# Score products over 128 rows: padding a 64-row contraction with zeros

## The chip, the core and the metric

The kernel runs on one core of a Trainium2 chip. A core has a matrix engine (TensorE, PE in the profile, with its weight loads as PEld), a vector engine (VectorE, DVE), a scalar engine (ScalarE, ACT), a general engine (GpSimd, POOL) and a sync engine (SyncE, SP) that here issues most of the DMAs. Each has its own queue of instructions and runs it in order; semaphores tie the queues together. The metric is the time on the device in microseconds (us), as the median of three executions. The profile is of one execution of its own.

## The reference

Two layers on an image batch x of 4 x 512 x 32 x 32, in float32. Each normalises its input over groups of channels and adds its output to it.

Layer 0 is a state-space mixer over the 1024 positions. Layer 1, in which the change lies, is attention over positions between two 3x3 convolutions:

```python
x_top = _conv(x, w_top, b_top, 0)           # 512 -> 64 channels, 1x1
x_center = _conv(x, w_center, b_center, 0)  # 512 -> 64 channels, 1x1
x_bottom = _conv(x, w_bottom, b_bottom, 1)  # 512 -> 512 channels, 3x3
sp_map = einsum('bnp,bpm->bnm', x_center^T, x_top)   # p: 64 channels
sp_map = softmax(sp_map over all n and m)
sp_map = einsum('bnm,bmc->bnc', sp_map, x_bottom^T)
out = _conv(x + sp_map.reshape(...), w_out, b_out, 1)
```

The score product is the first einsum: per image a 1024 x 1024 matrix, contracted over the 64 channels p.

## The kernel before

Layer 0 fills about the first 2190 us. A planner written in Python (`Plan`, with costs and due times) fixes its order; the change does not touch it, and its order on every engine stays as it was.

Layer 1 is written in program order and ordered by the compiler's scheduler. Its main loop (lines 1476 to 1488) runs over the four images b:

- `scores(0)` for the first image, once, ahead of the loop
- `conv3("b..")`: the bottom convolution, as a Winograd transform. Inputs `e`, `f`, `g`, `h`, `k`, `l` are made on ScalarE and GpSimd (lines 1331 to 1351), summed into `rr` and `v` on VectorE (1335, 1336, 1370 to 1373), and multiplied on TensorE with weights `uw` (line 1383, results `m_b`), which SyncE streams in 1 MB pieces through three buffers (line 1379). `n` (VectorE) and `y` (GpSimd, lines 1403 to 1418) gather the results
- `norm(b + 1)`: loads and normalises the next image, with the edges of its padded copy `xg` set to zero by GpSimd (lines 223 to 226)
- `attend`: scores times `y` (line 1431, `pat`), added to the image
- `scores(b + 1)`: the scores of the next image
- `conv3("o..")` (results `m_o`) and `finish`, the output convolution; `finish` loads the residual into `o` tiles (line 1457), transposes on TensorE (line 1464, `po`) and writes out (line 1474)

So the scores of image 0 stand ahead of its bottom convolution, and those of images 1, 2 and 3 ahead of the output convolution of the image before.

`scores` first makes both 1x1 convolutions in one product (line 1242, `pt`): 128 output rows, of which 0 to 63 are `top` and 64 to 127 `center`. ScalarE adds the biases and writes each into a tile of 64 partitions (lines 1247 and 1254); `center` comes from the upper half of PSUM into partitions 0 to 63. Then come 16 score products per image (line 1263, `psc`), each with 128 columns of `top` as weights and 512 columns of `center` streamed, over 64 rows. ScalarE copies each result to `st` (line 1267), VectorE takes row maxima `mx` (1268) and their maximum `mp` (1271), GpSimd the maximum over partitions (1273), and ScalarE the exponentials (1277).

`top` and `center` take two of three buffers of one ring, "f4" in the pool `l1f`; the `o` tiles of `finish` (128 partitions, the same length) share it. So a `top` or `center` of image 2 or 3 waits until an `o` tile has been written out, and an `o` tile until the score products that read `top` or `center` are done. A buffer costs the same space per partition whether a tile uses 64 partitions or 128.

Of the kernel before, what the change touches and what calls it, by code (L numbers as in the profile page):

```python
# [8 lines left out]
F32 = mybir.dt.float32  # L9
AF = mybir.ActivationFunctionType  # L10
# [5 lines left out]
P = 128  # L16
B, C, HH, WW = 4, 512, 32, 32
L = HH * WW
# [5 lines left out]
T = 512  # L24
NH = L // T
NB = B * NH
PAB = 64
# [143 lines left out]
def mamba_then_pab_kernel(  # L171
# [25 lines left out]
    nc = tc.nc  # L197
# [18 lines left out]
    pb_sb = cpool.tile([P, 1], F32, tag="pb", name="pb_sb")  # L216
# [952 lines left out]
    with ExitStack() as l1:  # L1169
# [5 lines left out]
        TI, TJ = HH // 4, WW // 2  # L1175
# [7 lines left out]
        fp = l1.enter_context(tc.tile_pool(name="l1f", bufs=3))  # L1183
# [50 lines left out]
        def scores(b, xg):  # L1234


            top = fp.tile([PAB, L], F32, tag="f4", name=f"top_{b}")
            center = fp.tile([PAB, L], F32, tag="f4", name=f"center_{b}")
            for h in range(NH):
                pt = ps.tile([P, T], F32, tag="ps", name=f"pt_{b}_{h}")  # L1240
                for c in range(NCC):
                    nc.tensor.matmul(
                        pt, wt_sb[:, c].rearrange("p j n -> p (j n)"),
                        xg[:, c, 1 + h * HR : 1 + (h + 1) * HR, 1 : WW + 1],
                        start=(c == 0), stop=(c == NCC - 1),
                    )
                nc.scalar.activation(
                    center[:, h * T : (h + 1) * T], pt[PAB:P], AF.Identity, bias=pb_sb[PAB:P]
                )
                tv = top.rearrange("p (r k i j) -> p r i j k", r=4, k=2, j=TJ)  # L1250
                pv = pt[0:PAB].rearrange("p (i r j k) -> p r i j k", r=4, j=TJ, k=2)
                hi = slice(h * TI // 2, (h + 1) * TI // 2)
                for r in range(4):
                    nc.scalar.activation(
                        tv[:, r, hi], pv[:, r], AF.Identity, bias=pb_sb[0:PAB]
                    )
            mx = spool.tile([P, NMC], F32, tag="mx", name=f"mx_{b}")
            st = []
            for m in range(NMC):
                t = xp.tile([P, L], F32, tag="st", name=f"st_{b}_{m}", bufs=NMC)  # L1260
                for h in range(NH):
                    pt = ps.tile([P, T], F32, tag="ps", name=f"psc_{b}_{m}_{h}")
                    nc.tensor.matmul(  # L1263
                        pt, top[:, m * P : (m + 1) * P], center[:, h * T : (h + 1) * T],
                        start=True, stop=True,
                    )
                    nc.scalar.copy(t[:, h * T : (h + 1) * T], pt)
                nc.vector.reduce_max(mx[:, m : m + 1], t, axis=AX.X)
                st.append(t)
            mp = spool.tile([P, 1], F32, tag="mp", name=f"mp_{b}")  # L1270
            nc.vector.reduce_max(mp, mx, axis=AX.X)
            ma = spool.tile([P, 1], F32, tag="ma", name=f"ma_{b}")
            nc.gpsimd.partition_all_reduce(ma, mp, P, bass_isa.ReduceOp.max)
            nc.vector.tensor_scalar_mul(ma, ma, -1.0)
            rs = spool.tile([P, NMC], F32, tag="rs", name=f"rs_{b}")
            for m in range(NMC):
                nc.scalar.activation(
                    st[m], st[m], AF.Exp, bias=ma, accum_out=rs[:, m : m + 1]
                )
            rp = spool.tile([P, 1], F32, tag="rp", name=f"rp_{b}")  # L1280
            nc.vector.reduce_sum(rp, rs, axis=AX.X)
            return st, rp
# [192 lines left out]

        xg = image[0]
        st, rp = scores(0, xg)
        for b in range(B):
            xb = conv3(f"b{b}", xg, ub, brow[0])
            after = norm(b + 1) if b + 1 < B else iter(())  # L1480
            next(after, None)

            v, chunk = by_chunk(f"o{b}", xg) if b + 1 == B else (None, None)
            attend(b, xg, st, rp, xb, after, chunk)
            if b + 1 < B:
                st, rp = scores(b + 1, image[b + 1])
            finish(b, conv3(f"o{b}", xg, uo, brow[1], v))
            xg = image.get(b + 1)
# [57 lines left out]
```

## Time and profile before

Three executions took 3271.97, 3272.30 and 3289.61 us. The profiled one took 3276.93, of which its trace spans 3275.1.

| part of the span | length us | PE busy | DVE busy | ACT busy | POOL busy | PEclk |
|---|---|---|---|---|---|---|
| to 2191 (layer 0) | 2191.0 | 1821.5 | 1651.9 | 1761.3 | 1978.4 | 0.92 |
| from 2191 (layer 1) | 1084.1 | 1051.0 | 540.1 | 146.1 | 286.2 | 0.95 |

How to read it: PEclk is the share of TensorE's full clock that was granted, averaged over the stretch. In layer 1 TensorE is busy 97% of the time, the other engines half of it at most. TensorE's waits there are few: 6.3 us before the score products of the four images together (for `top`), 5.1 before `po`, 4.1 before `m_o` (for `v_o`), 3.8 before `m_b` for weights.

### The profile page before, as it was taken

The numbers are of one execution on the slowest core, as the hardware profiler recorded it, in microseconds if no ns is written. First come the engines' busy times: TensorE is split into PE (matmuls) and PEld (weight loads), VectorE is DVE, ScalarE is ACT, GpSimd is POOL, SyncE is SP. The second block draws the span as 40 slices with busy tenths as digits, with TensorE's granted clock in tenths as the row PEclk, the third lists the DMA queues.
The fourth block names the chain that finished last, engine by engine and source line by source line (L and its number), as shares of the span: only waits on it lengthen the run. The fifth ranks groups of instructions, "written<-read, shape, count | busy, mean of one in ns | idle before, by whom it ended". The sixth has DMA issues, their size and how long they took to land.

```text
span 3275.1 us, 35019 instructions
## 1 busy us (share of the span) xinstructions
PE 2872.5 (88%) x11416; PEld 1688.1 (52%) x11416; DVE 2192.0 (67%) x1837; ACT 1907.4 (58%) x3589; POOL 2264.5 (69%) x1240
## 2 busy tenths in 40 slices
PE   5988688889778988888898978689999999999998
PEld 3545565555555655556655566554444444444443
DVE  3557788875888876789876599875365446447444
ACT  3389889996898986799998689752030030021000
POOL 7889989998899897899999799762142133224122
PEclk9889799999989998889999989798989989999999
DMA  7678868899778798968889888755438618808916
GB/s 231 172 269 311 272 213 269 282 317 323 272 242 264 270 304 293 326 224 262 283 292 324 293 302 284 219 203 214 166 137 314 241 59 310 324 32 299 327 72 251
DMA packets 388125, 823.81 MB, mean 252 GB/s; under 512 B 48360, under 2 KB 220136, under 8 KB 363368
## 3 DMA queue, kind: packets, MB, share of 16 engines
q1 hardware_dynamic: 378848, 806.01, 72.6%
q10 hardware_dynamic: 8936, 15.31, 1.3%
q8 instruction: 91, 1.49, 0.2%
q14 instruction: 90, 0.74, 0.1%
q0 software_dynamic: 160, 0.26, 0.0%
HBM read 720.28 MB, written 101.19 MB: 251 GB/s over the span
## 4 chain that ended last, share of the span: by engine, by line
PE 43%; POOL 22%; DVE 9%; DMA 8%; issue 7%; ACT 7%; SPq 0%; POOLq 0%; DVEq 0%; ACTq 0%
PE m_o L1383 10%; PE m_b L1383 9%; POOL da L818 7%; PE pat L1431 7%; POOL bbc L792 5%; PE y L826 4%; PE po L368 4%; POOL bbc L818 3%; PE psc L1263 3%; DVE da L806 2%; DMA bbc<-bcd 2%; ACT sc L763 2%; DVE bbc L806 2%; DMA cbc<-bcd 2%; DMA uw_b<-u_b 2%
## 5 line engine op out<-in xcount | busy, mean ns | idle before, releaser
L806 DVE TENSOR_TENSOR_SCAN da<-da,u 128x1024 f32<-128x1024 f32 x256 | 582.5, 2276 | 152.8 <-PE u L777 151.5
L763 ACT ACTIVATE sc<-dtxt,bt_sb 128x128 f32<-128x128 f32 x2048 | 633.2, 389 | 57.2 <-PE u L777 57.0
L792 POOL TENSOR_TENSOR bbc<-dtx,bbc 128x1024 f32<-128x1024 f32 x256 | 604.3, 2371 | 59.4 <-DMA bbc<-bcd 43.8
L818 POOL TENSOR_TENSOR da<-da,cbc 128x1024 f32<-128x1024 f32 x256 | 604.8, 2364 | 55.5 <-DVE da L806 48.0
L826 PE MATMUL y<-ident,da 128*128 128x128 f32 x2048 | 304.6, 296 | 127.1 <-POOL da L818 120.0
L826 PEld LDWEIGHTS y<-ident,da 128*128 128x128 f32 x2048 | 249.7, 152 | 238.6 <-POOL da L818 208.5
L806 DVE TENSOR_TENSOR_SCAN u<-u,bbc 128x1024 f32<-128x1024 f32 x128 | 292.2, 2283 | 103.3 <-ACT u L798 71.7
L826 PE MATMUL y<-ident,bbc 128*128 128x128 f32 x2048 | 303.0, 294 | 64.1 <-POOL bbc L818 38.0
L777 PE MATMUL u<-ident,sc 128*128 128x128 f32 x2048 | 300.7, 293 | 53.0 <-DVE da L806 33.9
L771 ACT ACTIVATE da<-dt,a_sb 128x1024 f32<-128x1024 f32 x256 | 290.5, 1140 | 92.0 <-PE y L826 91.3
L1383 PE MATMUL m_b<-uw_b,v_b 128*128 128x512 f32 x768 | 338.0, 598 | 6.8 <-DMA uw_b<-u_b 3.8
L1383 PE MATMUL m_o<-uw_o,v_o 128*128 128x512 f32 x768 | 339.0, 603 | 4.1 <-DVE v_o L1305 4.1
L806 DVE TENSOR_TENSOR_SCAN bbc<-u,bbc 128x1024 f32<-128x1024 f32 x128 | 291.8, 2280 | 55.5 <-ACT u L798 42.8
L826 PEld LDWEIGHTS y<-ident,bbc 128*128 128x128 f32 x2048 | 255.1, 152 | 126.5 <-POOL bbc L818 69.6
L818 POOL TENSOR_TENSOR bbc<-bbc,cbc 128x1024 f32<-128x1024 f32 x128 | 302.6, 2364 | 24.5 <-DVE bbc L806 22.1
L798 ACT ACTIVATE u<-dt,a_sb 128x1024 f32<-128x1024 f32 x256 | 284.6, 1112 | 54.5 <-DVE da L806 22.8
L777 PEld LDWEIGHTS u<-ident,sc 128*128 128x128 f32 x2048 | 255.9, 152 | 116.1 <-issue 37.6
L368 PE MATMUL pz<-xt,winc 128*128 128x512 f32 x512 | 249.2, 615 | 8.0 <-DVE xs L618 2.9
L1383 PEld LDWEIGHTS m_o<-uw_o,v_o 128*128 128x128 f32 x768 | 147.8, 193 | 195.6 <-issue 186.0
L1383 PEld LDWEIGHTS m_b<-uw_b,v_b 128*128 128x128 f32 x768 | 144.2, 191 | 194.5 <-issue 179.7
L1431 PE MATMUL pat<-y_b,st 128*128 128x512 f32 x512 | 221.7, 593 | 0.1
L1391 ACT ACTIVATE e_b<-m_b 128x512 f32<-128x512 f32 x24 | 14.3, 597 | 328.5 <-PE m_b L1383 299.3
(225 smaller groups left out, 4263.6 us busy)
## 6 DMA issues: line engine op xcount, KB each, us to landing
cbc<-bcd SPq DMA_DIRECT2D x512, 512.0 KB, 5.4
bbc<-bcd SPq DMA_DIRECT2D x256, 512.0 KB, 5.9
uw_b<-u_b SPq DMA_DIRECT2D x96, 1024.0 KB, 5.4
uw_o<-u_o SPq DMA_DIRECT2D x96, 1024.0 KB, 4.8
u_b<-work SPq DMA_DIRECT2D x192, 128.0 KB, 2.8
u_o<-work SPq DMA_DIRECT2D x192, 128.0 KB, 4.9
szd<-sz SPq DMA_DIRECT2D x32, 512.0 KB, 6.8
szl<-szd SPq DMA_DIRECT2D x32, 512.0 KB, 5.9
```

What stands on the lines that cost most here:

```text
L368: lambda k=k, lhs=lhs, rhs=rhs: nc.tensor.matmul(p()[:, :cols], lhs(), rhs(), start=(k == 0), stop=(k == n - 1)),
L763: nc.scalar.activation(sc()[:, k, :], dtxt()[:, k, :], AF.Copy, scale=bt()[:, k, s : s + 1],)
L771: lambda: nc.scalar.activation(da(), dt(), AF.Exp, scale=scale),
L777: nc.tensor.transpose(u()[:, k * P : (k + 1) * P], sc()[:, k, :], ident)
L792: "POOL", 2.38, lambda: nc.gpsimd.tensor_mul(dbx(), dtx(), b_bc()),
L798: lambda: nc.scalar.activation(da(), dt(), AF.Exp, scale=scale),
L806: lambda: nc.vector.tensor_tensor_scan(ht(), da(), dbx(), 0.0, ALU.mult, ALU.add),
L818: "POOL", 2.38, lambda: nc.gpsimd.tensor_mul(hc(), ht(), c_bc()),
L826: nc.tensor.matmul(y[h]()[:, k, :], hc()[:, at * P : (at + 1) * P], ident, start=(s == 0 and k == 0), stop=(s == NS - 1 and k == NK - 1), ...
L1263: nc.tensor.matmul(pt, top[:, m * P : (m + 1) * P], center[:, h * T : (h + 1) * T], start=True, stop=True,)
L1383: nc.tensor.matmul(m[q], v[:, q, k, c, :], w[:, c, :], start=(c == 0), stop=(c == NCC - 1 and not extra),)
L1431: nc.tensor.matmul(pt, st[m][:, 2 * P * j + h : 2 * P * (j + 1) : 2], xb[m // 2][:, m % 2, :], start=(m == 0), stop=(m == NMC - 1),)
```

## The change

The tiles `top` and `center` grow from 64 partitions to all 128. GpSimd sets their partitions 64 to 127 to zero, with two memsets of 64 x 1024 at the head of each `scores`: eight in all. ScalarE still writes the lower halves. The score product at line 1263 is unchanged in its text, but now contracts over 128 rows, the upper 64 of which add zero times zero. It is meant to make these products use all rows of the array.

```diff
@@ def scores(b, xg):
-            top = fp.tile([PAB, L], F32, tag="f4", name=f"top_{b}")
-            center = fp.tile([PAB, L], F32, tag="f4", name=f"center_{b}")
+            top = fp.tile([P, L], F32, tag="f4", name=f"top_{b}")
+            center = fp.tile([P, L], F32, tag="f4", name=f"center_{b}")
+            nc.gpsimd.memset(top[PAB:P, :], 0.0)
+            nc.gpsimd.memset(center[PAB:P, :], 0.0)
...
                 nc.scalar.activation(
-                    center[:, h * T : (h + 1) * T], pt[PAB:P], AF.Identity, bias=pb_sb[PAB:P]
+                    center[0:PAB, h * T : (h + 1) * T], pt[PAB:P], AF.Identity, bias=pb_sb[PAB:P]
                 )
-                tv = top.rearrange("p (r k i j) -> p r i j k", r=4, k=2, j=TJ)
+                tv = top[0:PAB].rearrange("p (r k i j) -> p r i j k", r=4, k=2, j=TJ)
```

`PAB` is 64, `P` 128, `L` 1024, `T` 512. With the change, the built program keeps the order of TensorE. On GpSimd the eight memsets come in: three ahead of `f_b` of the first image, one ahead of its partition maximum, and those of images 2 and 3 in pairs between lines 1404 and 1410. On SyncE the loads of `o_0` move from the output convolution into the bottom convolution before it. On ScalarE `e_b` of the first image goes ahead of its first `center`.

## The prediction

> **What bounds the kernel now.** I began with the shares of the chain that ended last: TensorE carries 43% of the span, the score products (`psc`) 3% of it.
>
> ```profile
> PE 43%; POOL 22%; DVE 9%; DMA 8%; issue 7%; ACT 7%; SPq 0%; POOLq 0%; DVEq 0%; ACTq 0%
> ```
>
> Then the group of line 1263, which holds 128 records for 64 products, so a product is two.
>
> ```profile
> L1263 PEld LDWEIGHTS psc<-center,top x128: 182/329/334, 2212.5 to 2936.7; 64*128 64x128 f32 x128
> L1263 PE MATMUL psc<-center,top x128: 589/1054/1057, 2212.5 to 2937.2; 64*128 64x512 f32 x128
> ...
>   ACT st L1267: 51.2, 62
> ```
>
> The same instruction takes 589 ns or 1054 ns, and its weight load 182 or 334: the ratio of a clock, not of a wait. ScalarE, which evicts, waited 51.2 us in all for these products, so they set the pace. The busy time by stage, one row per image, gives the cause (time; busy PE, PEld, ACT; PEclk):
>
> ```profile
> 2212.48:2237.78 25.30, 25.30 (x32) 9.58 (x32) 8.70 (x15) 0.55 0.24 102
> 2389.73:2414.79 25.06, 25.05 (x32) 9.44 (x32) 8.78 (x15) 0.55 0.00 0
> 2656.23:2681.56 25.33, 25.32 (x32) 9.45 (x32) 8.78 (x15) 0.55 0.00 0
> 2923.76:2937.76 14.00, 14.00 (x32) 5.90 (x32) 8.78 (x15) 1.00 0.00 0
> ```
>
> Three stages of four fall to the half clock; the last, with the same 32 records, keeps the full one. What a stage costs end to end is in the chain: from the first score product to the transposes of the output convolution behind it.
>
> ```profile
> 2656.23 25.32 PE psc L1263 x32
> ...
> 2770.83 1.31 PE po L1464 x10
> ...
> 2923.76 14.00 PE psc L1263 x32
> 2937.76 7.06 PE m_o L1383 x16
> ...
> 3024.82 1.31 PE po L1464 x10
> ```
>
> 114.60 us for the third image, 101.06 for the fourth. So 13.5 us per slow stage are real time: 11.3 in `psc` itself and 2.2 in the 16 records after it, which start at the half clock too (9.27 against 7.06).
>
> **What the skill says.** "TensorE: Matmul & The Clock Gate", Part 1: the array runs at 4/8 or 8/8 of its clock, set by its activity in free-running windows of 3413 ns. The trace agrees: the weight loads lengthen at about 2215.2, 2392.5 and 2658.9 us, and 177.3 and 266.4 are 51.95 and 78.1 such windows. That rows weigh in it is my reading of the trace. The windows that brought the drops held 0.5 to 0.8 us of idle array and 2.7 to 2.8 of 64-row work: at half weight 1.35 to 1.4 us of 3.41. The window of the fourth image that did not drop (2921.7 to 2925.1) held 1.26 idle, 1.34 of 64 rows and 0.8 of 128 rows: 1.47. Unweighted, it was the least busy of them all. Same page, "Why this matters for your kernels": a matmul of few rows takes the time of one with 128. Agreed: 589 against 592 ns at full clock. "GPSIMD Engine Reference", § 4.1: one-input work on GpSimd is roughly line-rate. "SBUF — State Buffer", Who interferes with whom: a two-input VectorE instruction contends with GpSimd work that reads SBUF, not with work that only writes. The first half shows here (`rr` of line 1335 takes 3.61 us beside a GpSimd subtraction, 1.29 alone); the second no run shows yet.
>
> **Do zeros count as activity?** The nearest thing in this trace is the first layer's transposes against an identity, whose columns hold 127 zeros of 128. Of these alone:
>
> ```profile
> 702.39:705.80 3.41, 3.41 (x32) 1.00 0.94 223
> 866.21:869.62 3.41, 3.41 (x16) 0.50 0.54 190
> 869.63:873.04 3.41, 2.32 (x17) 0.94 0.46 175
> ```
>
> They hold the full clock, and a window of them alone brings it back from the half. So I take it that rows addressed count, whatever is in them. It isn't proof: there only one operand is sparse.
>
> **The change part by part.** *Removed:* the half clock in `psc` and behind it. Second and third images: 2 x 13.5 = 27.0 us, measured on the fourth image, whose instruction order is theirs (VectorE, which becomes busy 14 of 14 us there, stops nobody). Fourth: 0, already at the full clock.
>
> *First image:* psc would end at 2212.48 + 14.0 = 2226.5 instead of 2237.8, but here the convolution behind it needs `v_b`, which hangs on GpSimd:
>
> ```profile
> 2218.54 2.28 POOL L1334 TENSOR_TENSOR f_b<-f_b,xg 128x1088 f32<-128x1088 f32 x1
> ...
> 2220.85 1.29 DVE L1335 TENSOR_TENSOR rr_b<-e_b,f_b 128x1088 f32<-128x1088 f32 x1 [4.46 <-POOL f_b L1334]
> ...
> 2229.33 2.51 DVE L1370 TENSOR_TENSOR v_b<-rr_b 128x1024 f32<-128x1024 f32 x1
> ```
>
> The built order of the changed kernel puts three of the new memsets before `f_b` on GpSimd (both of image 0 ahead of `e_b`, that of `top_1` ahead of `g_b`). *A memset of 64x1024:* the edge memsets of 128x136 follow one another by 0.15 us, 1.1 ns an element, so 1.15 us; low 0.85 (line rate at 1.2 GHz, the skill), high 3.2 (the strided edge, 0.40 us for 128). Queue: 2208.4 + 2.3, `e_b` to 2213.0, edges 0.9, `top_1` to 2215.0, then g, h, f 7.3: `f_b` ends at 2222.3, 1.5 us later than before. VectorE then does, in its order, rr 1.25, two maxima 2.25, rr 1.25, two maxima 2.4 (the `st` tiles are there by then): `v_b` at 2229.5, finished between 2230.9 and 2233.6, as GpSimd's `k_b` falls behind or before it. The convolution starts 4.2 to 6.8 us sooner. TensorE has then stood idle over 4 us, and the trace shows records at 0.50 clock after an idle of 2.58 us (2191.13), so the 2.2 us of slow start remain. Gain 5.5 us; 2 if memsets cost 3.2, 9 if the clock holds.
>
> *Other added work:* the remaining five memsets. That of `center_1` stands before the partition maximum (line 1273), which waits 2 us and more for VectorE's `mx` chain anyway. Those of `top` and `center` for images 2 and 3 stand after line 1404 and wait for the output DMAs of `o` tiles; behind them on GpSimd is `y_b` (line 1410), which starts at 2535.7 after 31.4 us of idle, while the last-but-one output was issued by 2509 and lands in 3.2 us median. Hidden. ScalarE moves `e_b` ahead of `center` in image 0: same sum before the first score product. *Moved on SyncE:* the load of `o_0` (512 KB) goes from the output convolution into the bottom one, between weight loads. In image 0 it meets an idle DMA. In images 1 and 2 it waits for the output of `o_3`, issued at 2517.7 and so landing by some 2521; the weight load behind it can't go before its slot at 2524. It adds 512 KB to a stretch moving 324 GB/s where single slices reach 480: 0 to 1 us each, taken as 0.
>
> Sum: 27.0 + 5.5 = 32.5 us. From the median of 3272.3 that is 3239.8, right at the 1% mark (3239.6). One doubt: the profiled execution took 3276.9, 4.6 more than the median. If that is profiling, 3239.8 stands. If it is a window more of half clock in each low stage (1.7 us each), the timed gain is 28 and the time 3244. I say 3240.
>
> **Rivals.**
> *Zeros are no activity.* The clock falls as before, the products are no faster, and the memsets hide: 3272, 3275 with the later `f_b` showing. Against it, the identity transposes.
> *The first image gives nothing back*, GpSimd and VectorE setting its end: 27 us, 3245. For it: `v_b` was ready only 6 us before its use.
> *A fourth low stage in the timed runs* (one of the three, 3289.6, lies 17 above the others): 4 stages, 46 us at most, 3226.
> *Slower: head-of-line waits.* GpSimd or SyncE blocked on output DMAs, in images 1 and 2, by as much as the longest such wait in the trace (SyncE at line 1457, 17.1 us), with the clock not recovered: 3272 + 34 = 3306. Against it: 20 us of slack on GpSimd, 3 on SyncE.
>
> **How the numbers follow.** The main case 0.64, half of it under 3239.6; fourth low stage 0.12; first image gives nothing 0.10; zeros inert 0.10; head-of-line 0.04. Faster by 1%: 0.32 + 0.12 = 0.44; within: 0.32 + 0.10 + 0.10 = 0.52; slower 0.04. The range, 3224 to 3250, takes in the first three cases (0.86).
>
> **What would show it.** `psc` near 590 ns in all four stages, PEclk 1.00 there, stages of 14.0 us; 101 us from `psc` to `po` in images 1 to 3; in image 0 an idle TensorE of 4 to 7 us before `m_b`, released by `v_b`; memsets of about 1.2 us. Wrong if `psc` records of about 1054 ns remain, if GpSimd's memsets run 3 us, or if SyncE shows new waits at line 1457 with TensorE waiting for `uw_b` behind them.

## The result, and the profile after

Four executions of the changed kernel beside four of the one before gave medians of 3240.52 us (3235.91 to 3248.82) and 3274.17 (3271.97 to 3289.61): a ratio of 0.9888, 95% interval 0.9857 to 0.992. In two later sets, on other executions, the ratio was 0.9924 (0.9898 to 0.9951) and 0.9907 (0.9872 to 0.9941). So the medians give a gain of 28 to 34 us, close to 1%. The ratios here and below are reckoned from all executions and so differ a little from the ratios of the medians; by them the gain is 25 to 37 us.

The profiled execution spans 3237.8 us against 3275.1, and its mean granted TensorE clock is 0.947 against 0.931. First, as before, the shares of the chain that ended last:

```profile
PE 37%; POOL 25%; DVE 11%; DMA 11%; issue 10%; ACT 5%; SPq 0%; POOLq 0%; ACTq 0%; DVEq 0%
```

TensorE's share fell from 43 to 37%. The group of the score products, now line 1266 (times in ns: min/median/max):

```profile
L1266 PEld LDWEIGHTS psc<-center,top x128: 186/190/191, 2209.4 to 2900.7; 128*128 128x128 f32 x128
L1266 PE MATMUL psc<-center,top x128: 592/592/697, 2209.5 to 2901.1; 128*128 128x512 f32 x128
```

Before, the median was 1054 ns. Now the longest record has 697 ns and none is at the half clock. The four stages, the 16 score products of one image each, have one row each (window; its length; busy time of PE, PEld, DVE, ACT and POOL, each with the number of records in brackets; PEclk; DMA share; GB/s):

```profile
2209.48:2223.45 13.97, 13.97 (x32) 5.97 (x32) 6.10 (x6) 10.19 (x19) 8.97 (x9) 1.00 0.42 176
2376.97:2390.97 14.00, 14.00 (x33) 6.36 (x34) 13.96 (x7) 9.49 (x18) 10.14 (x7) 1.00 0.00 0
2631.36:2645.36 14.00, 14.00 (x33) 6.36 (x34) 13.97 (x7) 9.49 (x18) 10.18 (x7) 1.00 0.00 0
2887.72:2901.72 14.00, 14.00 (x33) 6.36 (x34) 13.97 (x7) 9.49 (x18) 9.27 (x3) 1.00 0.00 1
```

Three stages went from about 25.2 to 14.0 us; the fourth was there already. VectorE, at 14 of 14 us in three of them, is now as busy as TensorE, but the length is that of 32 records at full clock, so VectorE stops nobody. In the chain of the second image, the first score product and the transposes behind the output convolution stand like this:

```profile
2376.97 14.00 PE psc L1266 x32
...
2477.84 1.31 PE po L1467 x10
```

That is 100.87 us, where the stages at half clock took 114.6.

The whole difference of the two profiled spans, piece by piece along TensorE:

| stretch | before | after | difference |
|---|---|---|---|
| to the first score product of image 0 | 2212.48 | 2209.48 | -3.00 |
| image 0: first score product to its use (`pat`) | 113.26 | 103.50 | -9.76 |
| image 0: `pat` to the scores of image 1 | 63.99 | 63.99 | 0.00 |
| image 1: first score product to `po` | 114.59 | 100.87 | -13.72 |
| image 1: `po` to the scores of image 2 (bottom convolution) | 151.91 | 153.52 | +1.61 |
| image 2: first score product to `po` | 114.60 | 100.88 | -13.72 |
| image 2: `po` to the scores of image 3 | 152.93 | 155.48 | +2.55 |
| image 3: first score product to `po` | 101.06 | 100.87 | -0.19 |
| image 3: `po` to the end | 250.28 | 249.21 | -1.07 |
| sum | | | -37.3 |

The first row is layer 0, which the change doesn't touch: in the kernels below its end moves between 2203.7 and 2215.2. So 37 us of gain stand in the score stages and 4 are given back in the bottom convolutions, if that isn't chance too. The 4 us of layer 0 and of the end belong to neither.

### The profile page after: what moved, and what is told of

It reads as the page before. It is cut to its first block, busy times and chain, and to the rows that moved or that the text cites. A ratio compares the mean times of both kernels' runs of the same rounds, so it can differ in the third digit from the quotient of the medians.

```text
span 3237.8 us, 35037 instructions
## 1 busy us (share of the span) xinstructions
PE 2820.9 (87%) x11416; PEld 1671.3 (52%) x11416; DVE 2198.1 (68%) x1837; ACT 1907.4 (59%) x3589; POOL 2274.3 (70%) x1248
## 4 chain that ended last, share of the span: by engine, by line
PE 37%; POOL 25%; DVE 11%; DMA 11%; issue 10%; ACT 5%; SPq 0%; POOLq 0%; ACTq 0%; DVEq 0%
PE m_o L1386 9%; POOL da L818 8%; PE m_b L1386 8%; PE pat L1434 7%; POOL bbc L792 5%; POOL bbc L818 4%; PE y L826 3%; DMA cbc<-bcd 3%; PE po L368 3%; DVE da L806 2%; DMA bbc<-bcd 2%; ACT sc L763 2%; DVE bbc L806 2%; DVE u L806 1%; PE u L777 1%
```

## The experiments

My theory: TensorE's clock falls when one of its free-running windows of 3.41 us holds too little activity. The rows that a product contracts over count in that activity, and 128 rows keep it up. Rivals: the gain comes from something else that the change moved (the memsets, `o_0`'s loads, the buffers), or 64 rows lose the clock whatever lies before them.

### The memsets without the products

The tiles, memsets and moved loads of the change stay, but the products read the lower 64 rows only (edit against the changed kernel).

```diff
-  pt, top[:, m * P : (m + 1) * P], center[:, h * T : (h + 1) * T],
+  pt, top[0:PAB, m * P : (m + 1) * P], center[0:PAB, h * T : (h + 1) * T],
```

> The changed kernel with its tiles, memsets and moved loads, but the score products read only the 64 lower rows of top and center. My theory (the gain is the clock alone, and rows addressed weigh in it): the half clock is back, psc records near 1054 ns in at least two images of the first three and stages of 24 to 25.3 us there; the cost of the additions shows by itself, the bottom convolutions of images 1 and 2 longer by 1.6 and 2.6 us as in the changed kernel, so 3273 to 3282 us. Rival (the gain comes from the new order of loads and of e_b, or from larger tiles): psc stages of 14 us or a time near 3240.

Measured: 3272.17 us beside 3271.99 of the kernel before, ratio 1.0002 (0.9966 to 1.0038). The stages of this kernel, same columns as above:

```profile
2204.42:2230.67 26.25, 26.25 (x33) 9.97 (x33) 14.06 (x11) 10.29 (x19) 13.97 (x10) 0.53 0.23 94
2381.61:2407.56 25.95, 25.95 (x33) 9.94 (x33) 25.41 (x16) 9.51 (x18) 10.09 (x7) 0.53 0.00 0
2649.92:2663.92 14.00, 14.00 (x33) 5.97 (x33) 13.96 (x7) 9.50 (x18) 10.08 (x7) 1.00 0.00 0
2906.38:2931.45 25.07, 25.07 (x33) 9.64 (x33) 25.04 (x16) 9.51 (x18) 9.21 (x3) 0.55 0.00 1
```

The half clock is back in three stages of four. But now it is the third image that escapes, and the fourth that falls. So the gain hangs on the rows that the products contract over. Which 64-row stage falls is not a property of the image: the same instructions meet the window at another phase, that is, they begin at another point of it. The memsets and the moved loads gain nothing that these runs would show; the interval is 12 us either way. I had expected 3273 to 3282, with the additions costing some 4 us; the median lies just under that, so their cost doesn't show in the time either.

### 64 rows, with no idle time ahead of them

The kernel before, with products over 128 rows, which nobody reads, between the 1x1 convolution and the score products: TensorE waits there for ScalarE to write `top`. At first it has two such products for each image.

```diff
+            pd = ps.tile([P, T], F32, tag="ps", name=f"pfill_{b}")
+            for c in range(2):
+                nc.tensor.matmul(
+                    pd, wt_sb[:, c].rearrange("p j n -> p (j n)"),
+                    xg[:, c, 1 : 1 + HR, 1 : WW + 1], start=(c == 0), stop=(c == 1),
+                )
             mx = spool.tile([P, NMC], F32, tag="mx", name=f"mx_{b}")
```

> The kernel before, 64 rows, no memsets; two products of 128 rows, whose result nobody reads, stand between the 1x1 convolutions and the score products and fill the idle of TensorE there (4 records, 1.7 us). My theory (a window drops the clock when idle time and half-weight rows fall together under some 1.4 of 3.41 us; 64 rows alone, 1.71, hold it): psc at 589 ns and stages of 14.0 us in all four images, some 36 us saved and 0.5 us per image spent, so 3235 to 3245 us. Rival (64 rows by themselves lower the clock, and the fourth image was luck): records of 1054 ns and stages of 24 us remain, 3272 to 3280 us.

Measured: 3240.11 us (3233.68 to 3246.65), ratio 0.9915 (0.9888 to 0.9941). Images 1 to 3 took 13.99, 13.99 and 14.00 us at clock 1.00. Image 0 still fell, with this row:

```profile
2208.63:2234.08 25.45, 25.45 (x33) 9.63 (x33) 14.08 (x11) 10.22 (x19) 13.34 (x6) 0.54 0.24 101
```

That was a miss: I had expected 14.0 us in all four. In image 0 `top` comes later, the fill ended at about 2207.8, and 0.82 us of idle time was left. The clock fell at 2210.9, so the window was 2207.49 to 2210.90 and held 0.31 us of 128 rows, 0.82 idle and 2.27 of 64 rows: with the 64-row work at half weight, 1.45 us. That lies right at the mark of about 1.46 us that windows of other traces show, further down. Then four products for image 0:

```diff
-            for c in range(2):
+            for c in range(NCC if b == 0 else 2):
```

> The kernel before with unread 128-row products ahead of the score products, four for image 0 and two for the others: no idle before any stage. Theory (64 rows hold the full clock when no idle of more than about 0.5 us lies in the same window): all four stages at about 14.0 us and clock 1.00, although they contract over 64 rows; image 0 gains some 9 us more than with two products, total 3229 to 3234. Rival (64 rows lose the clock by themselves in image 0, whatever lies before them): image 0 stays at 25 us and 0.55, total 3240 to 3243.

Measured: 3237.57 us (3233.79 to 3242.64), ratio 0.9906 (0.9881 to 0.9931); 3.6 us above the upper end of what I expected in time, with the stages as expected:

```profile
2207.57:2221.57 14.00, 14.00 (x33) 5.90 (x32) 6.44 (x6) 9.56 (x16) 9.08 (x5) 1.00 0.39 163
2375.53:2389.53 14.00, 14.00 (x34) 5.98 (x33) 13.96 (x7) 9.10 (x17) 9.73 (x7) 1.00 0.00 0
2628.76:2642.76 14.00, 14.00 (x34) 5.98 (x33) 13.96 (x7) 9.09 (x17) 9.72 (x7) 1.00 0.00 0
2882.80:2896.80 14.00, 14.00 (x34) 5.98 (x33) 13.97 (x7) 9.10 (x17) 8.84 (x3) 1.00 0.00 0
```

All four stages stand at the full clock over 64 rows. The rival falls: 64 rows hold the clock for 14 us, if no long wait stands ahead of them. What brings it down is the wait for `top` together with half-filled rows in the same window. Useless work in the wait gains what the zeros gain.

### 96 rows

The tiles end at row 96, with zeros on rows 64 to 95 (edit against the changed kernel):

```diff
-            top = fp.tile([P, L], F32, tag="f4", name=f"top_{b}")
-            nc.gpsimd.memset(top[PAB:P, :], 0.0)
+            top = fp.tile([96, L], F32, tag="f4", name=f"top_{b}")
+            nc.gpsimd.memset(top[PAB:96, :], 0.0)
```

and `center` alike.

> The changed kernel with tiles of 96 partitions, zeros on rows 64 to 95 only. My theory (activity is weighted by rows addressed): a window with 0.8 us of idle and 2.6 of 96-row work weighs 1.95 of 3.41 us, well over the 1.47 that held the clock before, so psc stays near 590 ns, 14.0 us a stage, some 3240 us. Rival (only products over all 128 rows count as activity): half clock in two or three images, stages near 25 us, 3270 us or more.

Measured, in a single execution: 3238.12 us. Images 1 to 3 stood at 14.00, 14.00 and 13.99 us and clock 1.00; image 0 at 15.67 us and 0.89, where I had expected 14.0. Around the start of image 0, TensorE alone (window; length; busy PE; PEclk; DMA share; GB/s):

```profile
2207.00:2210.30 3.30, 1.43 (x4) 1.00 1.02 403
2210.40:2213.70 3.30, 3.30 (x5) 0.50 1.02 429
2213.80:2224.40 10.60, 10.60 (x25) 1.00 0.09 36
```

A window of mostly idle time (1.42 us of 96-row work in it) brings the clock down at 2210.29, and after one window of 96 rows at half speed it is back at 2213.70: 3.41 us. 64 rows never came back in a stage of 25 us. A full window of 64 rows, 1.71 at half weight, holds the clock but doesn't raise it; one of 96 rows, 2.56, raises it.

### Memsets on VectorE

Both memsets on VectorE, the rest as changed:

```diff
-            nc.gpsimd.memset(top[PAB:P, :], 0.0)
-            nc.gpsimd.memset(center[PAB:P, :], 0.0)
+            nc.vector.memset(top[PAB:P, :], 0.0)
+            nc.vector.memset(center[PAB:P, :], 0.0)
```

> Both memsets on VectorE, the o_0 loads moved as in the changed kernel. Tells apart what the given-back 4.1 us hang on. If on the moved loads (SyncE waiting for the output of o_3, the weight load behind it): bottom convolutions of images 1 and 2 remain at about 153.5 and 155.5, total near 3240. If on GpSimd's queue (memsets waiting for buffers, y_b behind them): they fall back to about 151.9 and 152.9, total near 3236.

> Both memsets on VectorE, o_0 loads moved. If the moved loads cost 4 us as the first profile after suggested, it lies 3 to 4 us over the version with one memset on VectorE; if they cost 2 us or less on average, within 2 us of it, and some 6 us under the changed kernel.

Measured: 3232.42 us (3230.11 to 3249.06), ratio 0.99 (0.9866 to 0.9934); in a second set 3239.07 (3229.4 to 3243.17), 0.9889 (0.9857 to 0.9921). In the first profile the bottom convolutions of images 1 and 2 took 153.01 and 152.63 us, which spoke for GpSimd's queue; in the second 155.12 and 155.27, which speaks for the loads. Neither reading holds: one kernel gave both.

These two show besides that 128 rows with zeros don't withstand every gap. The first profile, TensorE alone:

```profile
2206.00:2209.10 3.10, 0.32 (x2) 0.99 0.87 283
2209.10:2212.50 3.40, 3.40 (x4) 0.51 1.02 422
2212.60:2216.00 3.40, 3.40 (x10) 1.00 0.71 299
```

The wait of 2.78 us for `top` fell almost whole into one window (2205.64 to 2209.05, with 0.67 us of work), the clock dropped at 2209.04, and it was back at 2212.46. The price was 15.66 us for the stage instead of 14.00. In the changed kernel a wait of 2.79 us at the same place cost nothing, because it lay across two windows:

```profile
2204.75:2208.16 3.41, 1.94 (x5) 1.00 0.93 262
2208.16:2211.57 3.41, 2.09 (x5) 1.00 1.01 416
```

The first holds the end of the 1x1 convolution, the second 2.09 us of score products. At half weight these would count 1.05, less than any window of 64 rows that held. So padding does two things: it keeps up a window with part of a gap, and where a window falls anyway, it raises the clock again after one window.

### One memset, and the loads back

With zeros in `center`, the upper rows of `top` may hold anything finite. Here the eviction writes `top` over all 128 rows (the upper ones get the values of `center`), and only `center` is zeroed: by GpSimd, and in a second kernel by VectorE. Without the first memset, the scheduler leaves `o_0`'s loads in the output convolution. The edit against the changed kernel, for GpSimd:

```diff
-            nc.gpsimd.memset(top[PAB:P, :], 0.0)
...
-                tv = top[0:PAB].rearrange("p (r k i j) -> p r i j k", r=4, k=2, j=TJ)
-                pv = pt[0:PAB].rearrange("p (i r j k) -> p r i j k", r=4, j=TJ, k=2)
+                tv = top.rearrange("p (r k i j) -> p r i j k", r=4, k=2, j=TJ)
+                pv = pt.rearrange("p (i r j k) -> p r i j k", r=4, j=TJ, k=2)
...
-                        tv[:, r, hi], pv[:, r], AF.Identity, bias=pb_sb[0:PAB]
+                        tv[:, r, hi], pv[:, r], AF.Identity, bias=pb_sb
```

> 128 rows as in the changed kernel, but only center is zeroed above row 63; top is evicted over all 128 rows of PSUM with the same instructions, so its upper rows hold the center values, which meet the zeros. Four memsets in place of eight, and the built order has the o_0 loads back in the output convolution, where the kernel before has them. My theory (the moved loads cost the bottom convolutions of images 1 and 2 their 1.6 and 2.6 us by holding the weight loads behind them): from po to the next psc 152 to 153 us again in images 1 and 2, psc 14.0 us everywhere, f_b of the first image 1.0 us sooner than in the changed kernel, 3 to 5 us faster than it, so 3233 to 3240 us. Rival (the 4 us come from the earlier start itself, DMA being the limit there): 153.5 and 155.5 us stay, the time at that of the changed kernel or 1 us under it.

> One memset only, on VectorE instead of GpSimd, and the o_0 loads in the output convolution as in the kernel before. Theory: nothing stands ahead of f_b on GpSimd, so v_b of image 0 comes about 1 to 2 us sooner and the idle before m_b falls from 3.6 to some 2 us; bottom convolutions of images 1 and 2 near 151.2; about 3231 (3228 to 3235). Rival: the memset on VectorE stands ahead of what v_b needs there, and image 0 gains nothing or loses 1 us: 3233 to 3236.

> One memset on VectorE, o_0 loads as in the kernel before. Theory: 3231 to 3235, 7 us or more under the changed kernel of the same call. Rival: within 3 us of it.

Measured: on GpSimd 3233.51 us (3228.52 to 3238.35), ratio 0.9901 (0.9869 to 0.9934). On VectorE 3233.08 (3230.23 to 3247.2), 0.9902 (0.9865 to 0.9939); in a second set 3240.34 (3230.09 to 3244.92), 0.9891 (0.9858 to 0.9924). All four stages take 14.0 us in each. The second set on VectorE lies above the 3231 to 3235 that I expected.

### The changed kernel again, beside these

> The changed kernel unaltered, beside its variants on the same chip. Theory (clock held in four stages; 4.1 us given back by the o_0 loads): 3238 to 3242, with bottom convolutions of images 1 and 2 at 153.5 and 155.5 us. If the difference from the version with one memset was the chip's or the execution's, it comes near that one's 3233.

> The changed kernel unaltered, in more rounds, to set it beside the two versions with memsets on VectorE. Theory (GpSimd's memsets put off v_b of image 0, the moved loads put off weight loads): 3238 to 3243, 7 to 9 us over both other versions. Rival (the differences of single executions are chance of DMAs and clock windows): all three within 3 us of each other.

Measured: 3242.04 us (3240.52 to 3250.8) and 3243.66 (3234.4 to 3249.18). In the last set the versions on VectorE lie 3.3 and 4.6 us under it, not 7 or more, and the intervals overlap widely: neither is shown to be faster than the changed kernel. The first sets, 9 us apart, had misled me.

What of the differences is firm, and what is scatter, the traces say (us; the last column is the sum of the bottom convolutions of images 1 and 2):

| kernel | loads of `o_0` | image 0, scores to `pat` | bottom 1 + 2 |
|---|---|---|---|
| before | output conv. | 113.26 | 304.8 |
| two fills / long fill | output conv. | 113.05 / 103.57 | 305.9 / 305.2 |
| one memset | output conv. | 102.79 | 302.4 |
| one memset, VectorE, twice | output conv. | 101.43, 101.37 | 305.7, 310.9 |
| memsets alone | bottom conv. | 113.20 | 308.1 |
| 96 rows | bottom conv. | 105.07 | 307.2 |
| changed, three times | bottom conv. | 103.50, 103.34, 103.00 | 309.0, 311.4, 307.6 |
| memsets on VectorE, twice | bottom conv. | 101.16, 101.13 | 305.6, 310.4 |

Image 0 is firm: two traces of one kernel agree within 0.5 us, and memsets on VectorE save about 2. The bottom convolutions are not: one kernel differs from itself by 5 us. Over all kernels the moved loads have 308.5 us on average and the others 305.8, 2.7 apart, while the first group spreads over nearly 6 us and the second over more than 8.

Two things blur that column. A wait for weights can itself cost the clock: in the second trace of the changed kernel (311.4) and the second of one memset on VectorE (310.9) one window of each of these two convolutions ran at the half clock, in the first of the latter one window in all, 1.7 us lost each time; in the others none. And the column leaves out the output convolutions: with one memset on GpSimd those of images 0 and 1 took 102.0 us or more from the first score product to `po`, where those of the changed kernel took 100.87. In the chain GpSimd stands still there for 5.5 us, by the queue entries of the memset (line 1240), just ahead of the `y_o` that `po` needs; the cause stays open.

## Why the prediction came out

3240 was forecast and 3240.52 measured. The cause was the one named. That the number fits to half a microsecond is luck: two terms of the sum were off, in opposite directions, and later sets gained over 5 us less than the first.

**Zeros count as activity.** Right. The identity transposes had pointed to it; the stages at 14.00 us and their return after one window show it. The Trainium skill, in "TensorE: Matmul & The Clock Gate", "Why this matters for your kernels", prices few rows like 128; at equal clock that held again (588 ns over 64 rows after the fills, 592 over 128). What such a price leaves out is the clock itself: the same product over 64 rows had a median of 1054 ns here.

**Rows weigh in the windows.** Right, and by a wider margin than the prediction's figures, which were somewhat off: it placed the windows by the lengthening weight loads, up to 0.3 us late. In the profile the clock column itself places them. In the kernel before (window; length; busy PE; PEclk; DMA share; GB/s):

```profile
2211.50:2214.91 3.41, 2.43 (x6) 1.00 1.01 406
2214.91:2218.32 3.41, 3.41 (x5) 0.50 1.02 430
2655.24:2658.65 3.41, 2.42 (x6) 1.00 0.00 0
2921.48:2924.89 3.41, 2.15 (x6) 1.00 0.00 0
2924.89:2928.30 3.41, 3.41 (x9) 1.00 0.00 0
```

The windows that brought the drops held 2.43, 2.68 and 2.42 us of 64-row work, at half weight 1.21 to 1.34 and not 1.35 to 1.4. The one of the fourth image held 1.13 us of 64 rows and 1.02 of 128, which weighs 1.59 and not 1.47; unweighted it is the least busy. In the memsets without products the third image escaped with 3.11 us of 64 rows in its first window, 1.56 at half weight. Where only full rows work, as in the bottom convolutions, the mark is at the same place: 1.46 us of work lost the clock (one memset on VectorE, first line), 1.45 kept it in another trace (memsets on VectorE, second line). That is as fine as a window can be placed.

```profile
2747.71:2751.12 3.41, 1.46 (x4) 1.00 0.98 406
2491.73:2495.14 3.41, 1.45 (x4) 1.00 0.96 400
```

With this mark, the window of image 0 that fell behind two fill products (0.31 us of 128 rows, 2.27 of 64) and the one of 3.11 us that held give an estimate for the weight of 64 rows: 0.46 to 0.51 of that of 128. In layer 0 even products without idle time lose it when they have 32 rows, as in the second trace of the changed kernel:

```profile
168.34:171.75 3.41, 3.41 (x8) 1.00 0.79 208
171.75:175.16 3.41, 1.72 (x3) 0.50 0.82 245
```

That every number of rows weighs by its share isn't shown, and busy time is not the measure for every instruction: 1.69 us of the short transposes `po` in one window lost the clock (two fill products, 3228.08 to 3231.49).

**Images 1 and 2: 2 x 13.5.** Measured 13.72 each. The rest of 0.2 shows in the fourth image too, which kept the clock before.

**Image 0: 5.5.** Measured 9.76, above the 9 I gave if the clock held. The failed step is "TensorE has then stood idle over 4 us ... so the 2.2 us of slow start remain". The first convolution products and what they waited for, in the changed kernel:

```profile
2205.16 0.95 POOL L1240 MEMSET top<- 64x1024 f32 x1 [14.78 <-issue]
2206.05 0.95 POOL L1241 MEMSET center<- 64x1024 f32 x1
...
2210.24 0.95 POOL L1240 MEMSET top<- 64x1024 f32 x1
...
2216.25 2.29 POOL L1337 TENSOR_TENSOR f_b<-f_b,xg 128x1088 f32<-128x1088 f32 x1
2218.57 1.29 DVE L1338 TENSOR_TENSOR rr_b<-e_b,f_b 128x1088 f32<-128x1088 f32 x1 [5.21 <-POOL f_b L1337]
...
2225.49 1.51 DVE L1373 TENSOR_TENSOR v_b<-rr_b 128x1024 f32<-128x1024 f32 x1
...
2227.06 3.27 PE L1386 MATMUL m_b<-uw_b,v_b 128*128 128x512 f32 x7 [3.61 <-DVE v_b L1373]
```

The wait is there, released by `v_b` as forecast, though a little shorter than the 4 to 7 us, but 3.61 us of idle time did not bring the clock down: the first 16 records took 7.2 us and not 9.27. It lay across two windows, and each kept more work than the mark:

```profile
2221.82:2225.23 3.41, 1.63 (x4) 1.00 0.20 28
2225.23:2228.64 3.41, 1.58 (x4) 1.00 0.33 126
```

Whether a wait costs 2.2 us is a matter of phase, and of the rows ahead of it: after the long fill, one of 2.12 us at the same place did (16 records in 8.83 us). It fell whole into one window, with 1.29 us of work, 1.04 of it over 64 rows. That is 2.1 of the 4.3 us. The rest is the earlier start: the first `m_b` begins 17.58 us after the first score product, where the forecast had 18.4 to 21.1 and the kernel before 25.3. The memsets took 0.95 us instead of the 1.15 estimated, so `f_b` ended 9.06 us after the first score product, where it was 8.34 before and 9.8 forecast; and `v_b` was done 8.5 us behind that, where I had allowed 8.6 to 11.3. The Trainium skill, in "GPSIMD Engine Reference", § 4.1, has work with one input at roughly line rate; a memset has no input, but the low estimate made from that, 0.85 us, was nearer to the 0.95 measured than the spacing I took.

**Moved loads: "0 to 1 us each, taken as 0".** Too low for the profiled execution, which gave back 1.61 and 2.55. The chain of the changed kernel in image 1 shows the way:

```profile
2483.94 7.15 DMA o<-x
...
2492.56 7.56 DMA out_dram<-o
...
2500.26 0.32 SPq L1460
...
2500.68 6.10 DMA uw_b<-u_b
...
2506.92 38.02 PE m_b L1386 x88
```

SyncE's load of `o_0` waits until `o_3` is written out, and the weight load stands behind it. I had placed that output at 2521 in the old trace, 3 us before the weight load's slot, and so called it hidden. It isn't: the output took 7.56 us here, where I had reckoned with the median of 3.2. TensorE's waits for weights in layer 1 of the changed kernel (us in total, times, longest):

```profile
PE m_b L1386 <- DMA uw_b<-u_b: 7.0, 7, 2.8
```

The kernel before had 3.8 us. The version with one memset on VectorE and no moved load, in its second set:

```profile
PE m_b L1385 <- DMA uw_b<-u_b: 8.6, 8, 2.3
```

This kernel has no such chain and yet more waiting. So the chain is real, but what it costs is not settled: 2.7 us on average by the table, within the scatter of the weight loads.

**The doubt about 4.6 us.** The profiled gain was 37.3 us, the timed ones 33.7, 28.0 and 28.2. The image 0 term of 4.3 too little, and the given-back 4.2, cancelled within the trace. What the trace gained beyond the 32.5 forecast is 3.0 us of layer 0 and 1.1 at the end, which the change has no part in as far as the runs show, and 0.6 in the other score stages. Why the timed gain is smaller would be plain if the kernel before has three low stages in some executions and fewer or more in others: its times run from 3244 to 3297, and the two traces of 64-row products without a fill kept the clock at different images. But only profiled executions show their stages, so this stays an inference.

**The rivals.** Zeros inert: fell. Image 0 gives nothing: fell. A fourth low stage: neither trace of 64 rows without a fill had it; but the fourth image can fall, as the memsets without products show. Head-of-line waits: their place was right (line 1460, `uw_b` behind it), their size of 34 us was not. The clock recovered.

## What to carry to other kernels

Where the same instruction has two durations at a ratio near two, look at the granted clock of its stage and then at what stands ahead of it: a short wait and half-filled rows together lose the clock, either alone may not. Rows of zeros, or unread work in the gap, are two ways to hold it, and each can gain no more than the half clock costs on the path (here 13.7 us per image at most). And before believing a gain or loss of a few us, trace one kernel twice: here the same stretch differed from itself by 5.

## What was not expected of the hardware

- The clock has two marks. In layer 1, with products of 512 columns, it fell in windows with up to about 1.46 us of work, 64 rows counted half, and stayed above that; 64 rows without a gap held it for 14 us. To come back took more: 25 us of 64 rows never raised it, nor did a window that weighs 2.5 (kernel before, 2412.89 to 2416.30); one of 96 rows, 2.56, did (2210.29 to 2213.70), and one of 128 rows as well (2209.04 to 2212.46).
- 3.61 us of idle TensorE, more than a window, left the full clock in place in one trace, spread over two windows; 2.12 us lost it in another, in one.
- A memset of 64 x 1024 float32 took 0.95 us on GpSimd and 0.91 on VectorE.
- The second half of what the prediction quoted on contention shows in the changed kernel: `v_b` of line 1374 took 1.30 us beside a memset on GpSimd (2229.45 to 2230.40), 1.22 undisturbed in the kernel before (line 1371 there), and its neighbour of line 1370 took 2.51 there beside a GpSimd subtraction.
